# Behind attention: every engine in the order of the source, and w_out prepared in steps beside matmuls

## Chip, core and metric

The kernel runs on one core of a Trainium2 chip. A core has five instruction queues: TensorE (PE, matmuls and transposes), VectorE (DVE), ScalarE (ACT), GpSimd (POOL) and SyncE (SP), which here starts the DMA transfers. [...] The metric is the time on the device in microseconds (us), the median of several runs; a profile of one execution shows where it goes.

## What is computed

Two layers over an image batch x of 2 x 56 x 56 tokens with C = 384 channels, all in float32. Layer 0 is neighbourhood attention (12 heads, 7 x 7 window) with a residual, then an MLP. Layer 1 is a depthwise 3 x 3 convolution with four exponential scans, projected back, then an MLP.

```python
# layer 0
x = x + attention(layer_norm(x) * g + b)
x = x + gelu(layer_norm(x) @ w1 + b1) @ w2 + b2          # 384 -> 1536 -> 384
# layer 1
p = layer_norm(x) @ w_in + b_in                          # 384 -> 768
local = depthwise_conv_3x3(p, k_conv)
lr, rl = ema_scan(local, axis=2), ema_scan(local, axis=2, reverse=True)
tb, bt = ema_scan(local, axis=1), ema_scan(local, axis=1, reverse=True)
mixed = 0.25 * (lr + rl + tb + bt) + local               # y = 0.6 * y_before + 0.4 * x
x = x + (layer_norm(mixed) * on_g + on_b) @ w_out + b_out
x = x + gelu(layer_norm(x) @ w1 + b1) @ w2 + b2
```

The norm over `mixed` is not applied to it. Instead `w_out` is prepared once: each row is multiplied by `on_g`, the mean of the rows is subtracted, and `on_b @ w_out` is added to `b_out`. The projection then needs only one factor per token, the inverse standard deviation.

## The kernel before, in words

**Attention** takes about the first 987 us and is not touched. It writes x1 (tokens by channels) to DRAM.

**First pass (the loop over `groups`).** The 6272 tokens are cut into a group 0 of 128 tokens and groups 1 to 12 of 512. For each group: twelve hidden columns (`hidden`: three matmuls by `w1` into `mm`, ACT applies GELU into `hid`); then, for the group before, `project_in`: transposes of its normalised x2, six columns by `w_in`, ACT evicts into `mx`, one store to `p_d`; then transposes of the next group's `xn` into `hT` (`channels`, evicted by ACT); then `tokens` per 128 rows: twelve matmuls by `w2` into `y`, which DVE adds to x as `xc`. Normalising a group takes DVE statistics (`st`, `mv`, `rs`), a power on POOL, a shift `sh` on DVE, and four ACT passes `xn`. In the first pass this is called for the next group at column m == 3 and 6, and for the waiting x2 (`normalize_x2`) at m == 2.

**Side work (the class `Beside`).** Convolution and scans run on DVE beside the matmuls. A `Band` job loads some lines of one 128-channel slice (`pt`), ACT writes the centre tap (`centre` into `loc`), DVE adds eight taps, stores `loc`, scans both ways along lines (`both`), and stores to `mix_d`. A `Columns` job loads `loc` for a whole image, ACT turns it (`turn` into `line`), DVE scans it both ways, and adds it to `mixed`, which is loaded from and stored to `mix_d`. Six Columns jobs follow an image's bands. Jobs are generators. After each piece of matmul work the source calls `beside.go(worth)`, which issues side steps until their planned time has used up `rate * worth` (rate 0.85, 1.0 for the second image). `beside.until(name)` issues all steps up to the end of a job at once. Some stores are issued one step late (`later`). Loads and stores all go through SP's queue.

**Last pass (the loop over `dgroups`).** Groups 0 to 11 have 512 tokens, group 12 has 128. `load_mix` loads `mx` (from `mix_d`) and x2. `measure` transposes `mx` on PE into `xi` for the statistics. `project_out` multiplies by `w_out`; DVE evicts with the factor and residual. Then hidden columns with `w1` of layer 1, and `tokens` by `w2`, an add and one store to `out` per 128 rows. Group g's hidden loop measures group g + 1. Group 6 (`half_way`) is the first that needs the second image, so behind group 4's `tokens` stand `beside.until((1, NI - 1))` and `load_mix(6)`; behind them stands `channels` for group 5. Ahead of the pass stand `beside.until((0, NI - 1))`, `load_mix(0)`, the last `project_in`, `measure` and `project_out` of group 0.

**Order.** The framework's scheduler decides how instructions stand on each engine. It takes the order of the source as priority, simulates when operands and buffers are ready by its own durations, and lets later instructions go ahead of earlier ones that it holds to be waiting. So the order on DVE, ACT and SP behind attention is the scheduler's and not that of the `go` calls.

Buffers that matter: three for `mm` (PSUM), two for `y`, three for transposes, two for `pt` and for Columns' `loc` together, two for `loc`/`line` of work, three for `both`/`mixed`.

Of the kernel before, what the change touches and what calls it, by code (L numbers as in the profile page):

```python
# [30 lines left out]
F32 = mybir.dt.float32  # L31
AF = mybir.ActivationFunctionType
ALU = mybir.AluOpType
# [4 lines left out]
B, H, W, C = 2, 56, 56, 384  # L38
NH, KS, HD = 12, 7, 32
P = 128  # L40
NC = C // P
INNER, NI = 2 * C, 2 * C // P
# [6 lines left out]
MT = NT * P  # L49
# [100 lines left out]
def block_kernel(ctx: ExitStack, tc: tile.TileContext, ins: dict, out: bass.AP):  # L150
    nc = tc.nc
# [24 lines left out]
    def col(name, i=0):  # L176
        return chan[:, COL[name] + i : COL[name] + i + 1]
# [56 lines left out]
    with ExitStack() as actx:  # L234
        wp = actx.enter_context(tc.tile_pool(name="a_w", bufs=1))
# [282 lines left out]
        project(w)  # L518


    wp = ctx.enter_context(tc.tile_pool(name="w", bufs=1))
    gp = ctx.enter_context(tc.tile_pool(name="g", bufs=NHID))
    io = ctx.enter_context(tc.tile_pool(name="io", bufs=2))
# [3 lines left out]
    ps_y = ctx.enter_context(tc.tile_pool(name="psy", bufs=2, space=PSUM))  # L527
# [17 lines left out]
    def load_group(src, group, tag):  # L545
        t0, n = group
        t = io.tile([P, NT, C], F32, name=tag)
        nc.sync.dma_start(
            out=t[:, :n, :], in_=src[t0 : t0 + n * P, :].rearrange("(k p) c -> p k c", p=P)
        )  # L550
        return t
# [29 lines left out]
    w_out = wp.tile([P, NI, C], F32, name="w_out")  # L581
    nc.sync.dma_start(out=w_out, in_=ins["L1_conv_w_out"].rearrange("(c p) n -> p c n", p=P))

    def row(name):
        return rows[:, 1 if name == "b_out" else 0, :]

    def add_row(x, n, name):

        engine = nc.vector if beside.busy() else nc.gpsimd
        engine.tensor_tensor(  # L590
            x[:, :n, :], x[:, :n, :], row(name).unsqueeze(1).to_broadcast([P, n, C]), ALU.add
        )
# [13 lines left out]
    def prepare_w_out():  # L606


        wide = gp.tile([P, MT], F32, name="wide", tag="hid")[:, :P]
        ps = ps_y.tile([P, C], F32, name="y")  # L610
        for c in range(NI):
            nc.vector.tensor_copy(wide, col("L1_conv_on_b", c).to_broadcast([P, P]))
            nc.tensor.matmul(ps, lhsT=wide, rhs=w_out[:, c, :], start=c == 0, stop=c == NI - 1)
        nc.vector.tensor_tensor(row("b_out"), ps, row("b_out"), ALU.add)
        ps = ps_y.tile([P, C], F32, name="y")
        mean = gp.tile([P, MT], F32, name="mean", tag="hid")[:, :P]
        nc.vector.memset(mean, 1.0 / INNER)
        for c in range(NI):
            nc.vector.tensor_scalar_mul(w_out[:, c, :], w_out[:, c, :], col("L1_conv_on_g", c))
            nc.tensor.matmul(ps, lhsT=mean, rhs=w_out[:, c, :], start=c == 0, stop=c == NI - 1)  # L620
        for c in range(NI):
            nc.vector.tensor_tensor(w_out[:, c, :], w_out[:, c, :], ps, ALU.subtract)

    def normalized(norm, x, n):
        xn = io.tile([P, NT, C], F32, name="xn")
        norm.apply_by_scalar(x, n, xn)
        return xn

    def channels(xn, n, g, b):
        hT = io.tile([P, NC, MT], F32, name="hT")  # L630
        to_channels(ps_t, [xn[:, k, :] for k in range(n)], hT, NC, g, b)
        return hT

    def columns(w, m, hT, n):

        ps = ps_m.tile([P, MT], F32, name="mm")
        for c in range(NC):
            nc.tensor.matmul(  # L638
                ps[:, : n * P], lhsT=w[:, c, m * P : (m + 1) * P], rhs=hT[:, c, : n * P],
                start=c == 0, stop=c == NC - 1,  # L640
            )
        return ps

    def hidden(w1, m, hT, n, b1):
        ps = columns(w1, m, hT, n)
        t = gp.tile([P, MT], F32, name="hid", tag="hid")
        nc.scalar.activation(t[:, : n * P], ps[:, : n * P], AF.Gelu, bias=col(b1, m))  # L647
        return t

    def tokens(lhs, w, k):  # L650

        ps = ps_y.tile([P, C], F32, name="y")
        for m, t in enumerate(lhs):
            nc.tensor.matmul(  # L654
                ps, lhsT=t[:, k * P : (k + 1) * P], rhs=w[:, m, :],
                start=m == 0, stop=m == len(lhs) - 1,
            )
        return ps
# [164 lines left out]
    def norm_of(x, n):  # L823
        norm = Norm(sm)
        for k in range(n):
            norm.add(k, [x[:, k, :]])
        return norm
# [9 lines left out]
    waiting = None  # L837
    bands = [(b, lo, hi) for b in range(B) for lo, hi in BANDS[b]]

    def project_in(g, xn):  # L840
        t0, n = groups[g]
        hT = channels(xn, n, "L1_conv_n1_g", "L1_conv_n1_b")
        pt = io.tile([P, NI, MT], F32, name="mx")
        for m in range(NI):
            ps = columns(w_in, m, hT, n)
            nc.scalar.activation(
                pt[:, m, : n * P], ps[:, : n * P], AF.Identity, bias=col("L1_conv_b_in", m)
            )
            beside.go(PRO)
        for b, at, here, n in images(t0, n * P):  # L850
            nc.sync.dma_start(
                out=p_d[b][:, :, at : at + n].rearrange("m p t -> p m t"),
                in_=pt[:, :, here : here + n],
            )
        if t0 + groups[g][1] * P > T1:
            beside.rate = 1.0
        while bands and bands[0][0] * T1 + min(bands[0][2] + 1, H) * W <= t0 + groups[g][1] * P:
            b, lo, hi = bands.pop(0)
            beside.jobs += [Band(b, m, lo, hi) for m in range(NI)]
            if hi == H:  # L860
                beside.jobs += [Columns(b, m) for m in range(NI)]

    def normalize_x2(g, x2, norm):

        t0, n = groups[g]
        xn = normalized(norm, x2, n)
        early = min(max((dgroups[half_way][0] - t0) // P, 0), n)
        if early:
            add_row(x2, early, "b_out")
        nc.sync.dma_start(  # L870
            out=x2_d[t0 : t0 + n * P, :].rearrange("(k p) c -> p k c", p=P), in_=x2[:, :n, :]
        )
        return g, xn

    for g, (t0, n) in enumerate(groups):
        hid = []
        for m in range(NHID):
            hid.append(hidden(w1, m, hT, n, "L0_conv_b1"))
            if m == 3 and g < last:
                x_next, n_next = xs.pop(g + 1), groups[g + 1][1]  # L880
                norm_next = norm_of(x_next, n_next)
                norm_next.close(n_next)
            if m == 2 and waiting is not None:
                waiting = normalize_x2(*waiting)
            if m == 6 and g < last:
                xn_next = normalized(norm_next, x_next, n_next)
                add_row(x_next, n_next, "b2_0")
            beside.go(MLP)
        if waiting is not None:
            project_in(*waiting)  # L890
        if g < last:
            hT = channels(xn_next, n_next, "L0_conv_ln2_g", "L0_conv_ln2_b")
        x2 = io.tile([P, NT, C], F32, name="xc")
        norm = Norm(sm)
        for k in range(n):
            ps = tokens(hid, w2, k)
            nc.vector.tensor_tensor(x2[:, k, :], ps, x[:, k, :], ALU.add)  # L897
            norm.add(k, [x2[:, k, :]])
            beside.go(ROW)
        norm.close(n)  # L900
        waiting = g, x2, norm
        if g == 0:
            prepare_w_out()
        if g + 2 <= last:
            xs[g + 2] = load_group(x1f, groups[g + 2], "xa")
        if g < last:
            x = x_next
# [55 lines left out]
    for g, (t0, n) in enumerate(dgroups):  # L963
        hid = []
# [12 lines left out]
        for k in range(n):  # L977
            ps = tokens(hid, w2, k)
# [74 lines left out]
```

## Time and profile before

| | |
|---|---|
| median of 3 runs | 3166.87 us (3166.78 to 3172.72) |
| profiled execution, its run | 3166.03 us |
| its span, granted PE clock | 3164.2 us, 0.972 |
| first hidden matmul behind attention | at 999.71 us |
| last `mixed` on DVE | at 2380.67 us |

How it reads by stage (us of busy time):

| stretch | length | PE | DVE | ACT | PE clock |
|---|---|---|---|---|---|
| 1000 to 1200 (first groups, no side work) | 200 | 199.10 | 34.74 | 58.78 | 0.98 to 1.00 |
| 1300 to 1500 | 200 | 191.12 | 144.48 | 55.03 | 0.99 |
| 1500 to 1700 | 200 | 174.66 | 179.75 | 69.07 | 0.95 |
| 2100 to 2300 | 200 | 169.95 | 185.94 | 54.32 | 0.92 |
| 2300 to 2500 | 200 | 182.36 | 95.03 | 45.23 | 0.94 |
| 2700 to 2900 | 200 | 200.00 | 33.10 | 29.59 | 1.00 |

A float32 matmul of the program shows as two records of PE, so twelve columns of three matmuls are 72 records. In the list of waits, "PE mm L638 <- ACT hid L647: 37.1, 12, 14.1" means that matmuls of line 638 waited 37.1 us in total, 12 times, 14.1 at most, for ACT's instruction of line 647. In a timeline the bracket behind an instruction is the idle time of its engine ahead of it and what ended it. Lines are those of the kernel before; in the changed kernel most stand 16 to 20 further down.

### The profile page before, as it was taken

What the parts mean: (1) busy time and instruction counts of PE and PEld (TensorE: products, weight loads), DVE (VectorE), ACT (ScalarE), POOL (GpSimd) and SP (SyncE); (2) the same over time, 40 slices, a digit from 0 to 9 for tenths busy, and PEclk for the clock granted to TensorE, in tenths of its full rate; (3) what the DMA queues carried; (4) which work ended last, traced back from release to release, by engine and by line L of the source; (5) the groups of instructions that cost most, each with busy time, mean ns of one, the idle gap of its engine ahead of it and who ended that gap; (6) DMA issues with size and microseconds to landing.
All of it is one profiled execution on the core that took longest, in us unless ns stands there. A gap on an engine that the chain in (4) does not pass through costs nothing.

```text
span 3164.2 us, 36023 instructions
## 1 busy us (share of the span) xinstructions
PE 2955.9 (93%) x13647; PEld 1612.7 (51%) x13647; DVE 1619.3 (51%) x3426; ACT 1061.3 (34%) x2506; POOL 330.9 (10%) x260
## 2 busy tenths in 40 slices
PE   6999999999997999999887899999779999999999
PEld 2555555555555555454443445455435555555555
DVE  3555555555464113939898892959982111111110
ACT  1555555555564222223334332222331111111111
POOL 2311022310031110000000000000000001111000
PEclk9999999999999999999998999999889999999999
DMA  6222222221124002313346331543551111111000
GB/s 139 72 62 60 64 58 72 66 64 52 57 65 147 28 36 71 120 62 135 119 148 243 139 126 64 184 155 135 198 203 61 40 40 40 40 40 40 18 10 13
DMA packets 130734, 275.87 MB, mean 87 GB/s; under 512 B 10192, under 2 KB 85440, under 8 KB 130560
## 3 DMA queue, kind: packets, MB, share of 16 engines
q1 hardware_dynamic: 130560, 273.57, 26.0%
q8 instruction: 107, 1.75, 0.2%
q14 instruction: 67, 0.55, 0.1%
HBM read 157.93 MB, written 115.61 MB: 86 GB/s over the span
## 4 chain that ended last, share of the span: by engine, by line
PE 61%; DVE 23%; DMA 5%; issue 5%; ACT 3%; POOL 2%; SPq 0%; POOLq 0%; ACTq 0%; DVEq 0%
PE y L654 20%; PE mm L638 19%; DVE loc L732 8%; PE pt L422 4%; PE tp L294 4%; PE tp L466 3%; PE sc L392 3%; PE tp L315 3%; PE o L439 2%; DVE line L679 2%; DVE both L679 2%; DMA xg<-in_x 2%; DVE both L683 2%; DVE line L683 2%; DVE st L192 2%
## 5 line engine op out<-in xcount | busy, mean ns | idle before, releaser
L638 PE MATMUL mm<-hT,w 128*128 128x512 f32 (+1 forms) x1872 | 791.2, 579 | 38.6 <-ACT hid L647 37.1
L654 PE MATMUL y<-w,hid 128*128 128x384 f32 x2352 | 775.5, 491 | 21.2 <-DVE xc L897 15.4
L654 PEld LDWEIGHTS y<-w,hid 128*128 128x128 f32 x2352 | 449.0, 192 | 332.8 <-DVE xc L897 19.1
L638 PEld LDWEIGHTS mm<-hT,w 128*128 128x128 f32 x1872 | 346.3, 194 | 439.0 <-issue 367.7
L408 ACT ACTIVATE pr<-pr,nm 112x238 f32<-112x238 f32 (+3 forms) x672 | 326.8, 488 | 232.2 <-DVE nm L401 229.5
L732 DVE SCALAR_TENSOR_TENSOR loc<-pt,taps,loc 128x990 f32<-128x990 f32 (+10 forms) x336 | 363.6, 1116 | 9.4 <-ACT loc L714 6.7
L647 ACT ACTIVATE hid<-mm,chan 128x512 f32<-128x512 f32 (+1 forms) x312 | 202.8, 659 | 461.2 <-PE mm L638 461.1
L401 DVE CUSTOM_DVE_ANT_0 pr<-sc,bias 112x238 f32<-112x238 f32 (+3 forms) x672 | 240.7, 408 | 171.0 <-PE sc L392 166.6
L200 POOL TENSOR_TENSOR rs<-rs,mhalf 128x4 f32<-128x4 f32 (+2 forms) x66 | 80.6, 1221 | 2029.8 <-DVE rs L197 1987.9
L638 PE MATMUL mm<-hT,w_in 128*128 128x512 f32 (+1 forms) x468 | 200.6, 588 | 32.2 <-ACT hT L229 26.4
L294 PE MATMUL tp<-hT,wqkv 128*128 128x448 f32 x504 | 208.9, 547 | 8.4 <-DVE qT L300 5.5
L422 PE MATMUL pt<-ident,pr 112*100 112x112 f32 (+5 forms) x1584 | 207.4, 270 | 9.8 <-ACT pts L427 9.8
L654 PE MATMUL y<-w_out,mx 128*128 128x384 f32 x588 | 199.5, 497 | 17.2 <-DVE xc L941 17.2
L229 ACT ACTIVATE hT<-tp,chan 128x512 f32<-128x512 f32 (+2 forms) x159 | 108.3, 743 | 303.3 <-PE tp L226 299.6
L422 PEld LDWEIGHTS pt<-ident,pr 112*100 112x100 f32 (+5 forms) x1584 | 161.0, 146 | 79.7 <-issue 53.6
L215 ACT ACTIVATE xn<-xc,sh,rs 128x384 f32<-128x384 f32 x98 | 62.5, 697 | 397.4 <-DVE sh L211 397.4
L897 DVE TENSOR_TENSOR xc<-y,xa 128x384 f32<-128x384 f32 x49 | 27.0, 552 | 293.4 <-PE y L654 293.4
L192 DVE BATCH_NORM_STATS2 st<-xi 128x6 f32<-128x384 f32 x98 | 50.3, 554 | 233.7 <-PE xi L929 233.6
L654 PEld LDWEIGHTS y<-w_out,mx 128*128 128x128 f32 x588 | 113.6, 195 | 99.1 <-DVE xc L941 19.1
L980 DVE TENSOR_TENSOR xc<-y,xc 128x384 f32<-128x384 f32 x49 | 27.2, 556 | 267.0 <-PE y L654 223.9
L638 PEld LDWEIGHTS mm<-hT,w_in 128*128 128x128 f32 x468 | 88.5, 197 | 140.2 <-issue 93.3
L392 PE MATMUL sc<-kT,qT 32*112 32x238 f32 (+3 forms) x1344 | 157.6, 417 | 0.0
(74 smaller groups left out, 2800.4 us busy)
## 6 DMA issues: line engine op xcount, KB each, us to landing
loc<-loc_d SPq DMA_DIRECT2D x24, 784.0 KB
mixed<-mix_d SPq DMA_DIRECT2D x24, 784.0 KB
mix_d<-mixed SPq DMA_DIRECT2D x24, 784.0 KB
xa<-x_d SPq DMA_DIRECT2D x24, 768.0 KB
p_d<-mx SPq DMA_DIRECT2D x11, 1536.0 KB
mx<-mix_d SPq DMA_DIRECT2D x11, 1536.0 KB
pt<-p_d SPq DMA_DIRECT2D x18, 560.0 KB
xg<-in_x SPq DMA_DIRECT2D x14, 672.0 KB
```

The costliest lines, as they stand in the source:

```text
L192: nc.vector.bn_stats(st[:n, i, :], x)
L294: nc.tensor.matmul(ps, lhsT=wqkv[:, c, m * P : (m + 1) * P], rhs=hT[:, c, :], start=c == 0, stop=c == NC - 1,)
L392: nc.tensor.matmul(ps[:, : w.nk], lhsT=qTs[w.b, w.g][d, hg, w.j, :], rhs=kT[d, hg, w.r0 : w.r0 + w.kr, w.c0 : w.c0 + w.kc], start=True, st ...
L401: nc.vector.tensor_tensor_reduce(out=self.pr[:, i, : w.nk], in0=ps[:, : w.nk], in1=w.bias[:, 4 * hg + i, : w.nk], scale=-1.0, scalar=BIG, ...
L408: nc.scalar.activation(self.pr[:, i, : w.nk], self.pr[:, i, : w.nk], AF.Exp, bias=nm[:, i : i + 1], scale=-1.0, accum_out=w.sums[:, h : h ...
L422: nc.tensor.transpose(tp[:n, i, :], self.pr[:, i, a : a + n], idt)
L638: nc.tensor.matmul(ps[:, : n * P], lhsT=w[:, c, m * P : (m + 1) * P], rhs=hT[:, c, : n * P], start=c == 0, stop=c == NC - 1,)
L647: nc.scalar.activation(t[:, : n * P], ps[:, : n * P], AF.Gelu, bias=col(b1, m))
L654: nc.tensor.matmul(ps, lhsT=t[:, k * P : (k + 1) * P], rhs=w[:, m, :], start=m == 0, stop=m == len(lhs) - 1,)
L679: nc.vector.tensor_tensor_scan(flat(dst), d, flat(src), 0.0, ALU.mult, ALU.add)
L683: nc.vector.tensor_tensor_scan(flat(dst)[:, ::-1], d, flat(dst)[:, ::-1], 0.0, ALU.mult, ALU.add)
L732: nc.vector.scalar_tensor_tensor(to, pt[:, lo + dy - self.top : hi + dy - self.top, xt : xt + n], self.tap(dy, dx), to, ALU.mult, ALU.add,)
```

## The change

Ahead of the pools of everything behind attention the source enters `tc.manual_schedule()`, to the end of the kernel: each engine's instructions then stand in the order in which the source issues them. The number and kinds of instructions stay the same.

`prepare_w_out` becomes a generator. It was called in one piece behind group 0's `tokens`; now one step is taken ahead of each hidden column of group 1. A step issues one matmul and the DVE copy for the next, first six steps for `on_b`, then six for the mean. `wide` gets two slots of its own and `mean` one, instead of slots among the `hid` buffers. All six scalings by `on_g` come in one piece between the two halves. In group 1 `normalize_x2` moves from m == 2 to m == 8, behind the new `b_out`.

```diff
+    ctx.enter_context(tc.manual_schedule())
     wp = ctx.enter_context(tc.tile_pool(name="w", bufs=1))
...
     def prepare_w_out():
-        wide = gp.tile([P, MT], F32, name="wide", tag="hid")[:, :P]
+        wide = wp.tile([P, 2, P], F32, name="wide")
+        mean = wp.tile([P, P], F32, name="mean")
+        nc.vector.memset(mean, 1.0 / INNER)
+
+        def spread(c):
+            nc.vector.tensor_copy(
+                wide[:, c % 2, :], col("L1_conv_on_b", c).to_broadcast([P, P])
+            )
+
+        ps = ps_y.tile([P, C], F32, name="y")
+        spread(0)
+        for c in range(NI):
+            yield
+            nc.tensor.matmul(
+                ps, lhsT=wide[:, c % 2, :], rhs=w_out[:, c, :], start=c == 0, stop=c == NI - 1
+            )
+            if c + 1 < NI:
+                spread(c + 1)
+        nc.vector.tensor_tensor(row("b_out"), ps, row("b_out"), ALU.add)
         ps = ps_y.tile([P, C], F32, name="y")
         for c in range(NI):
-            nc.vector.tensor_copy(wide, col("L1_conv_on_b", c).to_broadcast([P, P]))
-            nc.tensor.matmul(ps, lhsT=wide, rhs=w_out[:, c, :], start=c == 0, stop=c == NI - 1)
-        nc.vector.tensor_tensor(row("b_out"), ps, row("b_out"), ALU.add)
-        ps = ps_y.tile([P, C], F32, name="y")
-        mean = gp.tile([P, MT], F32, name="mean", tag="hid")[:, :P]
-        nc.vector.memset(mean, 1.0 / INNER)
+            nc.vector.tensor_scalar_mul(w_out[:, c, :], w_out[:, c, :], col("L1_conv_on_g", c))
         for c in range(NI):
-            nc.vector.tensor_scalar_mul(w_out[:, c, :], w_out[:, c, :], col("L1_conv_on_g", c))
+            yield
             nc.tensor.matmul(ps, lhsT=mean, rhs=w_out[:, c, :], start=c == 0, stop=c == NI - 1)
...
     for g, (t0, n) in enumerate(groups):
         hid = []
+        preparing = prepare_w_out() if g == 1 else iter(())
         for m in range(NHID):
+            next(preparing, None)
             hid.append(hidden(w1, m, hT, n, "L0_conv_b1"))
...
-            if m == 2 and waiting is not None:
+            if m == (8 if g == 1 else 2) and waiting is not None:
                 waiting = normalize_x2(*waiting)
...
             beside.go(MLP)
+        for _ in preparing:
+            pass
...
         waiting = g, x2, norm
-        if g == 0:
-            prepare_w_out()
```

## Prediction

> **What bounds the kernel now.** I read the busy table, then the waits from 1000 us (behind attention) on, then the stretches, then the timeline of TensorE (PE) with that of ScalarE (ACT) at the worst stall.
>
> ```profile
> PE 2955.9 (93%) x13647; PEld 1612.7 (51%) x13647; DVE 1619.3 (51%) x3426; ACT 1061.3 (34%) x2506; POOL 330.9 (10%) x260
> ```
>
> Who waited for whom: us in total, times, longest.
>
> ```profile
> PE mm L638 <- ACT hid L647: 37.1, 12, 14.1
> PE mm L638 <- ACT hT L229: 27.7, 6, 12.4
> PE y L654 <- DVE xc L941: 17.8, 4, 11.4
> PE y L654 <- DVE xc L897: 15.4, 6, 3.5
> ...
> ACT loc L714 <- DVE both L748: 135.1, 21, 21.4
> ACT line L779 <- DVE mixed L805: 98.0, 15, 16.4
> ...
> DVE mixed L805 <- DMA mixed<-mix_d: 2.6, 1, 2.6
> ...
> SPq L372 <- DMA x_d<-xr: 126.6, 53, 3.7
> ```
>
> Stretches: busy us (and instructions) of PE, weight loads, DVE, ACT, POOL, then PE clock, DMA share, GB/s.
>
> ```profile
> 1700.00:1900.00 200.00, 167.94 (x454) 84.52 (x453) 175.30 (x194) 67.09 (x94) 8.02 (x4) 0.91 0.41 151
> 1900.00:2100.00 200.00, 192.88 (x552) 99.51 (x552) 110.19 (x125) 52.14 (x76) 4.92 (x4) 0.98 0.35 123
> ...
> 2500.00:2700.00 200.00, 200.00 (x622) 108.68 (x621) 33.66 (x77) 34.70 (x51) 14.75 (x8) 1.00 0.09 33
> ```
>
> Timeline: start, length, instruction, in brackets the idle time before it.
>
> ```profile
> 1009.13 7.26 PE L654 MATMUL y<-w,hid 128*128 128x384 f32 x22
> ...
> 1730.36 1.31 ACT L215 ACTIVATE xn<-xc,sh,rs 128x384 f32<-128x384 f32 x2 [16.21 <-DVE sh L211]
> ...
> 1732.29 23.11 PE L638 MATMUL mm<-hT,w 128*128 128x512 f32 x48 [14.05 <-ACT hid L647]
> ...
> 1907.88 31.06 PE L638 MATMUL mm<-hT,w 128*128 128x512 f32 x72
> ...
> 2424.97 10.57 PE L638 MATMUL mm<-hT,w 128*128 128x512 f32 x24
> ```
>
> PE is the bound. The stretches say where it is not fed: full from 2500 us on, 168 of 200 us in 1700 to 1900, where VectorE (DVE) is busy for 175. The waits say how: PE waits for an ACT eviction, and ACT stands with `loc`, `line` or `xn` at the head of its queue, waiting for DVE. At 1730 ACT had waited 16.21 us for `sh`, with finished `mm` tiles behind it. DVE is not short of time overall (110 of 200 us in 1900 to 2100): the side work on it (bands and columns) comes in bursts.
>
> How much PE time is lost? Undisturbed pitches, from starts in the PE timeline: a hidden block 30.9, y of four rows 30.97, w_in 15.45, twelve transposes 1.31, one whole group 79.94 (1907.88 to 1987.82), one group of the last pass 81.5. Work from the first hidden matmul (999.71) to the hidden block of group 5 of the last pass: group 0 hidden and y 17.2, preparation 12 x 0.65 = 7.8, twelve hidden 370.8, twelve y 371.6, w_in 189.4, transposes 31.7, first measure, w_out and transposes 19.7, five last-pass groups 407.5: 1415.8 us. That hidden block starts at 2424.97 + 2 x 81.5 = 2588.0 us, so it took 1588.3. Lost: 172.5 us. The waits of PE sum to 125; the other 47.5 are matmuls at a reduced clock after a stall.
>
> [...] 48 matmul records after the 14 us stall took 23.11 us, undisturbed 20.9, so 2.2 us on top. [...] here the load burst of 1001 to 1013 us ran at 371 to 376, which I use.
>
> **The change part by part.** I use the order of instructions in both built programs.
>
> 1. *Source order in the steady passes.* Instruction counts are the same; only places move. Counted from the order and multiplied by the mean durations of the instruction groups, DVE has per group 49 to 59 us of side work (taps 1.24, scans 1.77 to 2.25, `mixed` 0.86 us each) and 11 to 12 of its own: 61 to 71 us beside 80 of PE. In the last pass 51 to 56 + 15 beside 81.5. In every part of a group (hidden, project, y) the DVE sum stays below PE's. So `sh` and evictions come at most some 5 us late, which three `mm` and two `y` buffers (2 x 2.58 and 7.7 us) take up. All 172.5 us lost go; I put 12 us back for small stalls (about one per group, 1 us).
>
> 2. *SP queue at the start.* Before, two of three w1 loads stood ahead of the last x1 store's wait; now the three stores, then `xa`, then all weights. The x1 store alone lands faster (in the chain of waits it took 5.43 us with loads beside it; the usual wait for such a store is 126.6/53 = 2.4), so hidden starts some 3 us earlier. But the 8.2 MB of loads begin where 1.6 MB were already moving. `xa` of group 1 is 6.7 MB in: 18 us at 372 GB/s, from 992.5, landing near 1010.5 (an estimate). And its twelve transposes now stand ahead of group 0's y, which started at 1009.13. Norm, pow, `xn`, transposes take 7.7 us: y starts near 1018. PE idles 11 us, 1.5 for the clock, minus 3: **+9.5**.
>
> 3. *w_out preparation.* Same 12 matmuls (7.8 us) and 12 DVE passes plus copies; now one matmul after each hidden column, operands ready 2.58 us ahead. It removes one 0.9 us wait. Two more SBUF tiles cost nothing. **0**.
>
> 4. *End of the first pass.* Before, early w_out matmuls filled the gap while group 12 was normalised (waits of 1.2 and 0.6 us). Now PE waits for eviction 0.6, stats 0.7, the last side step 5.2, rs and pow 1.3, sh 0.2, four `xn` 2.5, hT 0.5: 11, plus 2 clock. Then measure(0): eight DVE stats of 0.65 against 2.9 us of PE: 2.3. Then x3: 0.6 + 0.7 + 2.0 + 1.3 + 0.2 + 2.5 + 0.2 = 7.5, plus 2. **+24.8**.
>
> 5. *The flush in group 4 of the last pass.* Side work now keeps its planned pace, so it isn't done early (before: last `mixed` at 2380 us, in group 2). When `until` is called, seven half jobs of Columns are left: 7 x (4 scans 7.1 + 2 line ends 0.3 + 4 `mixed` 3.4) = 7 x 10.9 = 76 us, with 3 for DMA. On ACT, 32 `line` copies stand ahead of the three hT evictions of group 5. The last four can start when five half jobs are through (58 us after y's end), take 3.7: PE starts hidden at 62.5 instead of 1.5: 61, plus 2 clock. Four columns later (75) measure needs `mx`: DVE ends at 80.6, two stores 5, load 6: 92. 17, plus 1.5. **+81.5**.
>
> SP's order is otherwise late only where DVE or PE are as well; POOL's two swapped adds have 8 us of slack. Attention before 987 us is unchanged, and the tail behind the flush keeps its 576 us.
>
> Sum: -172.5 + 12 + 9.5 + 24.8 + 81.5 = -44.7. Against its own span, 3164.2 - 44.7 = 3119.5 us; times of runs stand 2.7 above that span (3166.87): **3122 us**, 1.4% faster.
>
> Unknown costs, both ends. Small stalls: 0 to 40 (40 being 3 us in each of 13 groups). Start: -3 (loads keep up) to 16. Flush: 61 (measure's wait hidden, DVE at its pure rate) to 100 (3 us wait per half job more). End of first pass: 15 to 32.
>
> **The rivals.**
>
> *A, slower: the columns starve.* In source order each Columns job on DVE goes scans, `mixed`, scans, `mixed`, and both the `mixed` load and the `line` copies are wanted early; the scheduler had put all scans ahead of them, and DVE waited 2.6 us in all. Say every job waits w on DVE. A group has about 14 us of DVE slack and 2.5 jobs: beyond w = 5.6 us PE stalls, in some 4.5 groups, and in the three flushed jobs w counts fully. With w = 11 (the longest ACT wait for such a load here was 11.0): 2.5 x 5.4 x 4.5 = 61, and 3 x 10 = 30 in the flush: 3122 + 91 = 3213. For: 800 KB loads behind 800 KB stores on one queue. Against: a `mixed` load landed 4.5 us after issue in the dense stretch at 2300, and DVE comes to it 3.7 us or more after issue.
>
> *B, the flush is cheap.* If ACT got to hT before the copies, 61 + 2 fall away: 3059. For: hT needs nothing of the columns. Against: the built order puts it behind all 32[...].
>
> *C, nothing.* If DVE were the true bound from 1225 to 2380 (90% in its bursts), stalls would only move, and the gain would equal the flush: 3160 to 3170. Against: DVE is busy for only 6 us in 1350 to 1400 and 16 in 1900 to 1975. That the order doesn't change is excluded by the built program.
>
> **How the numbers follow.** Forecast (3085 to 3155) 0.65; A 0.16; B 0.10; C 0.09, half of it in no change. The bounds above give 3122 - 12 - 12 - 20 - 10 and 3122 + 28 + 7 + 19 + 7 if all fell together, 3068 to 3183; taking B's upper part and A's lower part, I set 3075 to 3172. A measurement here tells about 0.2% (6 us) from no change. Faster: 0.65 + 0.10 + 0.03 = 0.78; same 0.05; slower 0.17.
>
> **What would show it.** Right: PE full in the stretches from 1120 to 1980 us at clock 0.98 or more; no PE wait on hid over 5 us there; a stall of about 60 us on hT near 2450 and one of about 17 on `mx` near 2520; y of group 0 starting near 1018. Wrong: PE waits for hid or xc spread over the passes (A), or no long stall near 2450 (B).

## Result and profile after

The changed kernel takes 3129.51 us (median of 4 runs, 3128.99 to 3132.55) beside 3166.82 us of the kernel before on the same chip: ratio 0.9885, 95% interval 0.9864 to 0.9907. Forecast were 3122 us and a range of 3075 to 3172. The profiled execution after has a span of 3130.7 us (before 3164.2).

Busy time of each engine, and the chain that ended last, from the page of the changed kernel:

```profile
PE 2930.5 (94%) x13647; PEld 1609.2 (51%) x13647; DVE 1664.2 (53%) x3426; ACT 1065.2 (34%) x2506; POOL 337.0 (11%) x260
...
PE 79%; DVE 7%; DMA 6%; ACT 3%; issue 3%; POOL 2%; SPq 1%; POOLq 0%; ACTq 0%; DVEq 0%
```

The work is the same, and yet PE's busy sum is 25.4 us smaller, because fewer matmuls run at a reduced clock (in 1700 to 1900 us the granted clock went from 0.91 to 1.00; in the 3.3 to 3.6 us behind each of the changed kernel's six long stalls, listed below, it was 0.50). PE's idle time, the span less the busy sum, fell by only 8.1 us (208.3 to 200.2): three quarters of the 33.5 us between the two profiled executions are matmuls that run faster. The chain that ended last now runs through PE for 79% of the span; before it was 61%, with 23% on DVE.

PE's waits behind attention, 985 to 3130 us (line, what it waited for, us in total, times, longest):

```profile
PE mm L654 <- ACT hT L229: 73.3, 9, 61.2
PE tp L226 <- ACT xn L215: 23.4, 3, 9.2
PE mm L654 <- ACT hid L663: 18.3, 5, 14.0
PE xi L947 <- DMA mx<-mix_d: 14.8, 1, 14.8
```

They sum to 129.8 us, nearly as much as before: 136.6, the prediction's 125 from 1000 us on and the 11.7 of the first transposes. But they are few and long. The waits for `xc` and `st` are gone, and of those for `hid` one long one and four of 1.5 us or less are left.

That they are few is most of the gain. PE's records show what a stall costs beyond its length: I took the starts of the matmuls in the 9 us behind each stall (or up to the next one), against the usual distance of two such matmuls (0.429 us with 512 columns, 0.323 us with 384). In these two kernels 1.6 to 4.2 us were lost behind stalls of 3 us or more, whether the stall was 3.06 us or 61.18, and 0.5 us or less behind stalls under 1.9 us; between 1.9 and 3 us some stalls cost it and some didn't. Behind 1000 us the kernel before has 19 stalls that cost 1.5 us or more, 39.0 us together, and the changed kernel six, 17.9 us together. The difference of 21.1 is most of the 25.4 us that PE's busy sum lost. (The prediction had its 47.5 us of slow clock as a remainder.)

The stretches show where PE is fed now (start and end, length, busy us of PE, weight loads, DVE, ACT, POOL, then PE clock, DMA share, GB/s):

```profile
1700.00:1900.00 200.00, 196.75 (x570) 101.84 (x569) 154.53 (x188) 91.77 (x128) 7.58 (x4) 1.00 0.51 187
...
2450.00:2550.00 100.00, 36.17 (x102) 19.14 (x100) 92.02 (x89) 33.12 (x41) 0.00 (x0) 0.68 0.49 183
```

The stretch 1700 to 1900 went from 168 busy us at clock 0.91 to 197 at 1.00. The price stands in the last line: the flush in group 4 of the last pass, with PE busy for 36 of 100 us and DVE for 92.

The six long stalls of PE behind its first transposes, with instructions of other engines that held the first and the fifth:

```profile
1008.45 0.56 DVE L192 BATCH_NORM_STATS2 st<-xa 128x6 f32<-128x384 f32 x1 [17.90 <-DMA xa<-x_d]
1009.41 0.99 POOL L592 TENSOR_TENSOR xa<-xa,rows 128x384 f32<-128x384 f32 x1 [19.05 <-DMA rows<-in_rows]
1012.74 2.50 ACT L215 ACTIVATE xn<-xa,sh,rs 128x384 f32<-128x384 f32 x4 [12.77 <-DVE sh L211]
1015.55 2.93 PE L654 MATMUL mm<-hT,w 128*128 128x128 f32 x12 [13.97 <-ACT hid L663]
...
2003.71 3.98 PE L226 MATMUL tp<-ident,xn 128*128 128x128 f32 x12 [8.10 <-ACT xn L215]
2050.20 3.98 PE L226 MATMUL tp<-ident,xn 128*128 128x128 f32 x12 [6.13 <-ACT xn L215]
2388.86 12.69 PE L654 MATMUL mm<-hT,w 128*128 128x512 f32 x24 [8.18 <-ACT hT L229]
2529.63 3.35 ACT L795 COPY line<-loc 128x392 f32<-128x392 f32 x4 [6.74 <-DVE mixed L821]
2533.71 13.64 PE L654 MATMUL mm<-hT,w 128*128 128x512 f32 x24 [61.18 <-ACT hT L229]
2562.19 1.51 PE L947 MATMUL xi<-ident,mx 128*128 128x128 f32 x6 [14.84 <-DMA mx<-mix_d]
```

From 1000 to 1012.7 us ACT stands at `xn` of group 1, with three finished hidden columns behind it. At 2529 it turns the last four pieces of `line`, and only then comes to `hT`.

Where the 33.5 us between the two profiled executions went, cut at instructions that both kernels have (hidden means the first hidden matmul of a group; the prediction's column takes its terms apart by stage):

| stretch | before | after | difference | predicted |
|---|---|---|---|---|
| attention, to the first transposes behind it, without their wait | 986.95 | 982.19 | -4.8 | 0 |
| wait of these transposes for `xn` | 11.74 | 9.16 | -2.6 | -3 |
| first hidden (999.71; 992.37) to hidden of group 2 | 95.0 | 112.4 | +17.4 | +11.5 |
| to hidden of group 0 of the last pass (2120.12; 2053.96) | 1025.4 | 949.2 | -76.2 | -78 |
| to hidden of group 5 (2588.06; 2533.71) | 467.9 | 479.7 | +11.8 | +7 |
| to the end | 576.1 | 597.0 | +20.9 | +18.5 |

(The predicted values: 172.5 lost before are 60.4 in the last pass, 467.9 against 407.5, about 1 in the head, and 111 between; 8 of the 12 us of small stalls and the 24.8 for the end of the first pass go to the fourth line, 4 of the 12 and the 63 to the fifth. The start's +9.5 is the second line and 12.5 of the third.) The first line is no effect of the change: among the kernels profiled in this study, whose instructions stand in the same order there, this time ran from 980.3 to 989.0 us.

### The profile page after: what moved, and what is told of

Read it like the earlier page. It is cut to its first block, busy times and chain, and to the rows that moved or that the text cites. A ratio compares the mean times of both kernels' runs of the same rounds, so it can differ in the third digit from the quotient of the medians.

```text
span 3130.7 us, 35981 instructions
## 1 busy us (share of the span) xinstructions
PE 2930.5 (94%) x13647; PEld 1609.2 (51%) x13647; DVE 1664.2 (53%) x3426; ACT 1065.2 (34%) x2506; POOL 337.0 (11%) x260
## 4 chain that ended last, share of the span: by engine, by line
PE 79%; DVE 7%; DMA 6%; ACT 3%; issue 3%; POOL 2%; SPq 1%; POOLq 0%; ACTq 0%; DVEq 0%
PE y L670 29%; PE mm L654 27%; PE pt L422 4%; PE tp L294 4%; PE tp L466 3%; PE sc L392 3%; PE tp L315 3%; PE o L439 2%; DMA xg<-in_x 2%; PE tp L226 2%; DMA mixed<-mix_d 1%; DVE loc L748 1%; ACT pr L408 1%; DVE st L192 1%; PE xi L947 1%
## 5 line engine op out<-in xcount | busy, mean ns | idle before, releaser
L670 PE MATMUL y<-w,hid 128*128 128x384 f32 x2352 | 762.9, 486 | 0.0
L748 DVE SCALAR_TENSOR_TENSOR loc<-pt,taps,loc 128x990 f32<-128x990 f32 (+9 forms) x336 | 377.2, 1123 | 17.3 <-ACT loc L730 8.9
L670 PE MATMUL y<-w_out,mx 128*128 128x384 f32 x588 | 191.8, 486 | 0.0
L427 ACT COPY pts<-pt 80x448 f32<-80x448 f32 (+3 forms) x228 | 117.4, 515 | 85.9 <-PE pt L422 85.9
```

The costliest lines, as they stand in the source:

```text
L427: nc.scalar.copy(t[:n], tp[:n])
L670: nc.tensor.matmul(ps, lhsT=t[:, k * P : (k + 1) * P], rhs=w[:, m, :], start=m == 0, stop=m == len(lhs) - 1,)
L748: nc.vector.scalar_tensor_tensor(to, pt[:, lo + dy - self.top : hi + dy - self.top, xt : xt + n], self.tap(dy, dx), to, ALU.mult, ALU.add,)
```

## The experiments

The theory at the start: the order of the source carries the gain, because side work in bursts on DVE had held ACT, and ACT PE; the new costs are the flush, the head and the end of the first pass. Rivals: the stepwise preparation carries it; the order of one engine alone does; the flush hides as soon as ACT reaches `hT` first. All times are medians of 4 runs (12 in the first) with ratios to the kernel before on the same chip, where it took 3165.87, 3165.49 and 3164.52 us in the three sets.

**One part of the change alone.**

```diff
 # steps, without the order
-    ctx.enter_context(tc.manual_schedule())
```

> The preparation of w_out in steps alone; the order of the engines is left to the scheduler as in the kernel before. Theory (the order carries the gain, the steps remove one wait of 0.9 us): within 6 us of the kernel before, 3160 to 3172 us, with PE waits of about 110 to 140 us behind 1000 us. Rival (the steps carry the gain): 3130 to 3145 us.

Measured: 3162.77 us, ratio 0.9987 (0.9978 to 0.9996). PE's waits, listed as above (lines of this kernel), are those of before:

```profile
PE mm L653 <- ACT hid L662: 39.5, 15, 15.3
PE mm L653 <- ACT hT L229: 27.5, 6, 12.2
PE y L669 <- DVE xc L958: 17.8, 4, 11.4
```

```diff
 # order alone: the kernel before, preparation in one piece behind group 0, and
+    ctx.enter_context(tc.manual_schedule())
     wp = ctx.enter_context(tc.tile_pool(name="w", bufs=1))
```

> Every engine in the order of the source, but the preparation of w_out in one piece behind group 0, as before. Theory: the gain of the order is whole; the piece now stands bare on PE, each of its first six matmuls waiting for a copy on DVE (0.23 us and the way between the engines), about 3 to 7 us more than the changed kernel: 3132 to 3138 us. Rival (the order alone is not enough): 3150 us or more.

Measured: 3138.19 us, ratio 0.9918 (0.9900 to 0.9936), 0.2 us above the range that was expected. In its trace the bare preparation waits 4.4 us in all (six times for `wide`, once for `w_out`). So the order carries the gain. The steps add little. Alone they took 3.1 us off the median, but only 0.4 off the profiled execution from the first transposes on (2165.6 to 2165.2). Within the order that part took 2143.3 us without them and 2139.4 in the changed kernel, 3.9 less, about the 4.4 of these waits; these medians are 9 us apart, but their intervals overlap.

**Which engine's order?**

```diff
-    ctx.enter_context(tc.manual_schedule())
+    ctx.enter_context(tc.manual_schedule(engines={mybir.EngineType.DVE}))         # one kernel
+    ctx.enter_context(tc.manual_schedule(engines={mybir.EngineType.Activation}))  # the other
```

> Source order on VectorE alone; the other engines as before in their order. Theory (bursts of Columns work on DVE ahead of the normalisation were the cause): the waits of the steady passes fall under 30 us, 3060 to 3150 us, lower than with all engines where the flush is spread. Rival (the order of ACT or of the queues carries the gain): 3150 us or more.

Measured: 3097.11 us, ratio 0.9783 (0.9768 to 0.9797), within what was expected.

> Source order on ScalarE alone; VectorE and the others as before in their order. Theory (bursts on DVE were the cause): the bursts and the waits on them stay, PE waits of 90 us or more, 3145 to 3180 us. Rival (ACT's order carries the gain): 3120 to 3140 us.

Measured: 3096.62 us, ratio 0.9785 (0.9770 to 0.9799), lower than both ranges. For ACT alone the theory fell: bursts on DVE were to keep PE waiting 90 us or more, and they do not. The bursts themselves are shorter, since the scheduler formed another order for DVE. Added up from DVE's records, the longest runs of side work between two instructions of the main work are 39.8, 35.1, 33.0 and 31.7 us ahead of the flush (before 59.7, 59.4, 50.8 and 48.9). PE is busy in all of 1120 to 1700 us.

PE's waits in the 860 us from 1120 to 1980, by what it waited for (us):

| order of the source on | for evictions by ACT | for `xc` by DVE | both |
|---|---|---|---|
| no engine (before) | 53.5 | 15.4 | 68.9 |
| DVE alone | 25.6 | 0 | 25.6 |
| ACT alone | 0.8 | 7.3 | 8.1 |
| all (the changed kernel) | 7.6 | 0 | 7.6 |

Each engine's own order took away all or nearly all of PE's waits for that engine, and half of those for the other.

What ACT itself waited for in that stretch, in the kernel before:

```profile
ACT xn L215 <- DVE sh L211: 152.9, 16, 31.9
...
ACT loc L714 <- DVE both L748: 97.2, 16, 21.4
...
ACT line L779 <- DVE mixed L805: 47.5, 8, 16.4
```

ACT's order alone (there is no line for `xn` or for `line` waiting on DVE at all):

```profile
ACT hid L663 <- PE mm L654: 406.5, 100, 31.5
...
ACT loc L730 <- DVE both L764: 26.4, 3, 9.5
```

DVE's order alone:

```profile
ACT loc L730 <- DVE both L764: 117.2, 17, 16.9
...
ACT xn L215 <- DVE sh L211: 75.6, 17, 32.0
ACT line L795 <- DVE mixed L821: 74.5, 9, 17.5
```

Before, the scheduler had put `xn`, `loc` and `line` on ACT ahead of where they could start, and ACT stood with them at its head for some 300 us, evictions behind them. In the source's order ACT mostly waits for matmuls. But the length of ACT's waits is not the measure of the harm: with DVE's order alone ACT stood at the same three for 267 us, nearly as long as before, and PE lost less than half as much (25.6 against 68.9 us). It matters whether PE needs an eviction just then.

A reading that fits is that a long stall needed both, side work in bursts on DVE and an ACT queue that had its dependents too early, so that either order alone takes most of it away. It is not shown: where one engine alone has the order of the source, the scheduler forms other orders for the rest, PE among them. How much each contributes by itself stays open.

Both kernels are also 33 us faster than the changed one, for three reasons in their traces. Behind the first transposes in the head neither has a wait over 2.2 us, where the changed one has 13.97. With DVE's order alone ACT evicts all twelve hidden columns of group 0 ahead of `xn`; with ACT's order alone ACT stands at `xn` for 7.53 us, as in the changed kernel, but PE's order is the scheduler's, and PE goes on with `y` of group 0 at 1004.48 us. Neither has the stall of 8.18 us at 2388. And their flush is cheaper: with ACT's order alone DVE begins the flushed columns beside the `w_out` and y matmuls of group 4 (16 of its `mixed` instructions are left behind the last y, 29 in the changed kernel; PE waits there for `xc`, 6.58 and 6.00 us), and the wait for `hT` is 37.37 us; with DVE's order alone ACT evicts `hT` and the hidden columns between the line copies, and only `mx` is waited for, 44.37 us.

**The flush.**

```diff
 # rate in the second image
-            beside.rate = 1.0
+            beside.rate = 1.15      # the other kernel: 1.05
```

> The changed kernel with the planned rate of the side work at 1.15 in place of 1.0 from the second image on, so that no half job of Columns is left when the last one is called for (7.25 are left at 1.0). Theory (the flush is the price: stalls of 61.2 and 14.8 us and some 3 us of slow clock): about 75 us less, less 0 to 20 us for a fuller DVE: 3052 to 3075 us, and no PE wait over 10 us between 2400 and 2600 us. Rival (DVE is the bound, stalls only move): 3115 us or more.

Measured: 3075.79 us, ratio 0.9722 (0.9704 to 0.9740), 0.8 us above what was expected. No long stall is left at the flush, but denser side work makes new ones, such as this, where ACT waits for the first Columns load of an image:

```profile
1708.63 0.91 ACT L795 COPY line<-loc 128x392 f32<-128x392 f32 x1 [7.33 <-DMA loc<-loc_d]
1718.78 3.78 PE L654 MATMUL mm<-hT,w_in 128*128 128x512 f32 x4 [11.27 <-ACT hT L229]
```

> Rate 1.05 in the second image: five half jobs of columns are left at the flush where the changed kernel has seven and a quarter. Theory (each half job left costs its DVE time, about 11 us): some 25 us less: 3102 to 3110 us. Rival (a cost of the flush whatever its length): 3122 us or more.

Measured: 3108.76 us, ratio 0.9822 (0.9808 to 0.9837). PE's two long waits in the timeline:

```profile
2507.84 12.96 PE L654 MATMUL mm<-hT,w 128*128 128x512 f32 x24 [32.21 <-ACT hT L229]
2536.69 1.51 PE L947 MATMUL xi<-ident,mx 128*128 128x128 f32 x6 [15.90 <-DMA mx<-mix_d]
```

Seven and a quarter half jobs left: 61.18 us on `hT`; five: 32.21; none: 0. That is 29.0 us for 2.25 half jobs, 12.9 each on this one wait; the medians are some 21 us apart, 9 each. The last five cost less each, as the prediction has it: ACT can turn its last lines while DVE still has two half jobs to do. The cost is the work that is left over.

```diff
 # hT of the next group evicted ahead of the flush
+        if g < last:
+            hT = channels(xn, dgroups[g + 1][1], "L1_conv_n2_g", "L1_conv_n2_b")
...
-        if g < last:
-            hT = channels(xn, dgroups[g + 1][1], "L1_conv_n2_g", "L1_conv_n2_b")
```

> The transposed rows of the next group are evicted ahead of the flush's line copies. Theory (the copies hold all of ACT, so the wait only moves to the next thing ACT has to do): the 61 us wait on hT becomes three hidden columns of work and then a wait on hid of some 50 us, the wait for mix grows to about 23 us, and nothing is gained: 3126 to 3134 us. Rival (only hT was late, and the flush hides beside the group's matmuls): the 61 us go, 3065 to 3080 us.

Measured: 3132.32 us, ratio 0.9894 (0.9877 to 0.9910). The two waits of the flush in PE's timeline:

```profile
2535.81 5.00 PE L654 MATMUL mm<-hT,w 128*128 128x512 f32 x6 [51.77 <-ACT hid L663]
2564.50 1.51 PE L947 MATMUL xi<-ident,mx 128*128 128x128 f32 x6 [23.68 <-DMA mx<-mix_d]
```

51.77 + 23.68 = 75.5 us, against 61.18 + 14.84 = 76.0: the wait moved to the next thing that ACT had to evict, and nothing was gained.

**The head.**

```diff
 # xa of group 1 ahead of w2 and w_in (w2 also goes ahead of w_in)
     w1, w2, s2 = load_w(0)
+    xs[1] = load_group(x1f, groups[1], "xa")
+    load_w2(w2, s2)
     w_in = wp.tile([P, NC, INNER], F32, name="w_in")
...
-    load_w2(w2, s2)
-    xs[1] = load_group(x1f, groups[1], "xa")
```

> The changed kernel with the load of group 1's x1 ahead of the loads of w2 and w_in. Theory (ACT stands at group 1's xn with finished hid tiles behind it until 6.7 MB have landed): x1 lands after 3.2 MB, the stall of 14.0 us in group 0's hidden columns and its slow clock (some 5 us) go: 3108 to 3116 us. Rival (the start is bound by w2 or by the norm chain): 3125 us or more.

Measured: 3132.07 us, ratio 0.9895 (0.9879 to 0.9910): nothing gained, as the rival had it. The timeline of DVE and POOL says why:

```profile
1000.40 0.56 DVE L192 BATCH_NORM_STATS2 st<-xa 128x6 f32<-128x384 f32 x1 [7.24 <-DMA xa<-x_d]
1010.65 0.99 POOL L592 TENSOR_TENSOR xa<-xa,rows 128x384 f32<-128x384 f32 x1 [17.68 <-DMA rows<-in_rows]
1012.65 0.16 DVE L211 SCALAR_TENSOR_TENSOR sh<-mv,rs 128x4 f32<-128x4 f32 x1 [9.29 <-POOL rs L200]
```

`xa` is there 8 us earlier, but the pow stands on POOL behind `add_row` of group 0, and that waits for the row `b2_0`, which is loaded behind the weights.

```diff
 # both loads ahead of w_in and w2
     w1, w2, s2 = load_w(0)
+    load_row(0, "b2_0")
+    xs[1] = load_group(x1f, groups[1], "xa")
     w_in = wp.tile([P, NC, INNER], F32, name="w_in")
...
     load_w2(w2, s2)
-    xs[1] = load_group(x1f, groups[1], "xa")
...
-    load_row(0, "b2_0")
```

> The row b2_0 and the rows xa of group 1 are loaded ahead of w_in and w2, so that neither VectorE's statistics nor POOL's add_row, which stands ahead of the pow, waits for weights. Theory (ACT's xn of group 1 waits for both loads, with finished hidden columns behind it): the 14 us wait at 1015 us and the slow clock behind it go but for about 3 us: 3112 to 3119 us. Rival (the xn is late for another reason, or w2 now lands too late for y): 3126 to 3134 us.

Measured: 3123.32 us, ratio 0.9871 (0.9857 to 0.9886), 4 us above what was expected. The wait on `hid` at 1011 us is 5.42 us instead of 13.97, and from the first transposes to the same hidden column further on (1286.81; 1292.57 in the changed kernel) it takes 291.2 us instead of 301.2: 10.0 less. So both loads were the holder, though 5.42 and not 3 us were left, as `xa` still arrived at 1003.78. The median is 6 us lower, but the intervals of the two ratios overlap: the medians alone don't show the gain, the trace does. (Attention ended 4.5 us later in that profiled execution than in the changed kernel's.)

**The end of the first pass.**

```diff
 # in the first pass and in project_out alike
             norm.add(k, [x2[:, k, :]])
+            if k == n - 1:
+                norm.close(n)
             beside.go(ROW)
-        norm.close(n)
```

> The normalisation's closing steps stand ahead of the last side step where the rows of the next group come last. Theory: the side step (3.4 us) is part of the two waits on xn at 2003 and 2050 us; they shrink from 8.1 and 6.1 us to about 4.7 and 4, with less of the slow clock behind them: 3122 to 3127 us. Rival (the statistics' own chain is all of it): no change, 3128 to 3131 us.

Measured: 3131.01 us, ratio 0.9892 (0.9878 to 0.9907): no gain that the median shows. Its timeline of DVE and POOL at the first of the two waits:

```profile
2002.58 0.16 DVE L197 SCALAR_TENSOR_TENSOR rs<-mv,ones 128x4 f32<-128x4 f32 x1
2002.66 2.25 DVE L699 TENSOR_TENSOR_SCAN both<-decay,both 128x1008 f32<-128x1008 f32 x1
2002.91 2.80 POOL L200 TENSOR_TENSOR rs<-rs,mhalf 128x4 f32<-128x4 f32 x1 [78.27 <-DVE rs L197]
2004.94 1.21 DVE L764 SCALAR_TENSOR_TENSOR both<-both,loc 128x1008 f32<-128x1008 f32 x1
2006.07 0.15 DVE L211 SCALAR_TENSOR_TENSOR sh<-mv,rs 128x4 f32<-128x4 f32 x1
```

The side step now stands ahead of `sh` instead of ahead of `rs`; only the pow went beside it. The two waits on `xn` went from 8.10 and 6.13 to 6.95 and 4.98 us.

**Both gains together.**

```diff
 # ACT's order alone, and rate 1.15
-    ctx.enter_context(tc.manual_schedule())
+    ctx.enter_context(tc.manual_schedule(engines={mybir.EngineType.Activation}))
...
-            beside.rate = 1.0
+            beside.rate = 1.15
```

> Source order on ScalarE alone, and rate 1.15 in the second image, so that nothing is left for the flush. Theory (the two gains add up, since one lies in the steady passes and the head, the other in the flush): 3097 less the 37 us wait, its slow clock and the wait of mix behind it: 3048 to 3062 us. Rival (the denser columns stall ACT or the normalisation, which VectorE now orders freely): 3070 us or more.

Measured: 3067.17 us, ratio 0.9690 (0.9674 to 0.9706). It beats both kernels, the changed one by 2.0%, but stays 5 us above what was expected. Beside ACT's order at rate 1.0, PE's waits behind attention fell from 96.0 to 59.8 us, the flush's among them entirely; the time from the first transposes on fell by 30.8 (2099.3 to 2068.5). That the two gains add is right in kind; where the last 5 us went was not found.

```diff
 # order on all engines, both loads of the head early as above, and
-            beside.rate = 1.0
+            beside.rate = 1.15
```

> Source order on all engines, rate 1.15 in the second image, and the loads of the first run of this set. Theory (the gains add up): 3076 less about 14 us: 3057 to 3065 us. Rival (w2 too late for y, or the wait moves): 3070 us or more.

Measured: 3070.59 us, ratio 0.9705 (0.9684 to 0.9725): above what was expected and within the rival's range. The rival's mechanism is not in the trace: the head's wait is 4.01 us, PE's other waits are those of rate 1.15 alone within 0.1 us, and the profiled execution (3065.89 us) is 8.3 us shorter than the one of rate 1.15 alone. But two of the four runs took 3074.92 and 3077.59 us; why is open. The interval of this kernel overlaps with that of the one before it and with that of rate 1.15 alone, so which is best is not told apart.

## Why the prediction was right, and where its steps were not

The forecast of 3122 us was 7.5 us low, and its case came in: the steady passes were fed, and the new costs stood where they were put. That it came so close is in part luck. In the profiled executions the part behind attention gained 28.7 us where 44.7 were forecast; another 4.8 came from attention, which the change doesn't touch, and the medians are 37.3 apart. By its own steps, in the profiled executions:

1. *Steady passes.* All 172.5 us came back but for small stalls, as put: PE is busy for 851.5 of the 860 us from 1120 to 1980 at clock 1.00, and no wait on `hid` there exceeds 1.6 us. Not in the sum was one stall of 8.18 us at 2388 with 2.1 us of slow clock behind it: the first Columns job of an image, whose `loc` load SP issues behind stores, while ACT stands at `line`. SP issued that load at 2374.34, behind stores whose data DVE had only just written; ACT had stood there since 2359. That is rival A's mechanism, once and not per job; its 2.5 jobs a group never starved (DVE waited 14.1 us for `mixed` in the whole kernel, 2.2 at most, where A needed more than 5.6 each). The cause as put, DVE's bursts, was not all of it: ACT's own order mattered too, and restoring either took most of the stalls away.
2. *Start.* Put at +9.5; measured +17.4 - 2.6 = +14.8. The estimate of the load was good (`xa` at 1008.45 against 1010.5, y of group 0 at 1020.83 against 1018). The holder was wrong: group 1's "twelve transposes now stand ahead of group 0's y", which were to hold PE; but PE never got that far. ACT's `xn` of group 1 stands between the hidden evictions of group 0, so PE stopped within group 0's hidden columns. And "POOL's two swapped adds have 8 us of slack" was wrong: in the changed kernel the first of them ended 1.1 us before the pow could start, in the run with `xa` early it held the pow, and only both loads together freed 10.0 us.
3. *Preparation, 0.* Nearly so: ratio 0.9987 for the steps alone, their two tiles with them. Within the order they save about 4 us by the traces.
4. *End of the first pass, +24.8.* Measured about 22: waits of 8.10 and 6.13; twice twelve transposes of 3.98 us instead of 1.47; 24 `xi` records of 3.97 instead of some 2.9; 36 records of w_in of 17.30 instead of 15.72. Here the waits were put too high (18.5 for the two) and the slow clock too low (4, measured about 8). The side step that was put into this wait is in it, but moving it brought only 1.2 us at each place.
5. *Flush, +81.5.* Measured 61.18 + 14.84 waiting, and with the slow clock some 82. The size is the prediction's best step. The stalls began at 2472.5 and 2547.4, 20 to 30 us later than put. By the run with five left a half job costs 12.9 us on `hT` rather than 10.9.

Rival B had the flush cheap if ACT reached `hT` first, "61 + 2 fall away". The run that does this shows the wait moving to `hid` and `mx`; with DVE's order alone ACT gets through, and `mx` still costs 44. Rival C, DVE as the bound, falls with rate 1.15: the same work of DVE, packed more densely, and 90 us off the kernel before.

The sum by these terms was -44.7, measured -28.7 behind attention (table: 17.4 - 2.6 - 76.2 + 11.8 + 20.9). Of the 16 between, some 6 are the start and 10 the stall at 2388; the rest cancels.

For what a stall costs beyond its length, the prediction put 1.5 to 2 us of slow clock, its author's estimate; it had read 2.2 us behind one stall of 14 us. In the changed kernel the granted clock was 0.50 in the 3.3 to 3.6 us behind each of the six long stalls, and four of them were followed by 2.1 to 3.1 us of slow matmuls (12.69 and 13.64 us for 24 records against 10.57, twice 3.98 for twelve transposes against 1.47). The six cost 2.2 to 4.2 us each in the 9 us behind them. From what length on a stall costs this was not shown: in the kernel before, PE idled for only 2.26 us ahead of 1326.49, its granted clock in the 3.6 us from there was 0.53, and 1.8 us were lost.

## What to carry to other kernels

Count the stalls of the bounding engine, not only their sum: here the sum of waits hardly changed, and most of the net gain came from 19 costly stalls becoming six. Where that engine waits for evictions, look at what the evicting engine stands at in that moment: in the kernel before, ACT stood for 16.21 us at an `xn` placed ahead of its input, with finished `mm` tiles behind it, and PE waited 14.05 us. Giving ACT alone the order of the source fed PE in the steady passes as well as giving it to all (8.1 and 8.5 us idle of 860). Work that is called for "all at once" makes somebody wait: putting one eviction ahead of it only moved the wait, and the two cheaper orders still left 37 and 44 us. Spread it ahead by a slightly higher pace, and look again, since the denser pace makes stalls of its own. Before a load is moved forward, follow every queue between it and the waiting engine: here the pow stood on POOL behind an add that waited 17.68 us for its row, and moving `xa` alone gained nothing.

## What was not expected of the hardware

A pow on POOL of 128 x 4 elements took 1.01 us where DVE was between side steps (2001.71 in the changed kernel) and 2.80 us beside a scan on DVE (2002.91 in the run with the closing steps first); it ended 0.8 us after the scan did. That the scan is the cause is not shown, and spans on POOL are rough. The side step behind the scan, beside which the pow still ran, took 1.21 us, its usual time (mean 1.20 in the changed kernel). And the length of attention, the same instructions in the same order in all these kernels, wandered by 8.7 us between executions (980.3 to 989.0), as much as several effects studied here.
